# A three-stage kernel on one core: alternating passes of a two-layer graph stage, and one-hot matrices kept in DRAM

## The chip, the core and the metric

The kernel runs on one core of a Trainium2 chip. Its time is the device time of one execution in microseconds (us), and the median of several executions is given. The core has five queues that matter here, each worked off in order. PE is TensorE, with its weight loads shown apart as PEld. DVE is VectorE, ACT is ScalarE, POOL is GpSimd, and SP is SyncE, which issues every DMA of this kernel. An instruction that waits holds up everything behind it on its own queue, and nothing on the others.

## The reference, cut to what matters

The input `x` is 16 graphs x 32 channels x 512 nodes in float32. Three residual parts follow one another: a graph part, a state-space scan, and a low-rank feed-forward part. Only the graph part is touched by the change.

```
keys   = 4 space-filling-curve keys of 3 coordinates (10 bits each)    # per graph
order  = argsort(keys), one order for each of 4 methods
neigh  = for each node i: the 10 nodes around place i in each order    # a window of the sorted list
layer(feats, perm, W_lin, W_conv):
    q      = [center, neigh - center] for 4 methods   -> 256 values per (node, neighbour), as float16
    attn   = softmax(q q^T / sqrt(32)) over the 10 neighbours, 8 heads
    fused  = (attn q) W_lin^T + b;  h = W_conv fused
    return max over neighbours of leaky_relu(instance_norm(h))
f1 = layer(f0, ...)         # 32 channels out
f2 = layer(f1, ...)         # 64 channels out
x += leaky_relu(instance_norm(W_conv3 [f0, f1, f2]))
```

The same orders serve both layers. In layer two only the features differ.

## The kernel before

**The stages.** `graph_part` is emitted first, under an order of work that is written out by hand, then `scan_part`, then `ffn_part`. Both later parts are the same in both kernels.

**The groups and the passes.** Sixteen graphs of 32 channels are four groups g of 128 partitions. A pass is one layer of one group, and there are eight of them in the list `order` (line 955). A pass goes through 43 blocks of 12 nodes (`NG`, `NGRP`). The loop at line 986 emits one block at a time, as a software pipeline: scores of this block, exponentials and sums of the block before, transposed shares and outputs of the block three before, the reduction over neighbours of the block four before, and the differences (POOL, lines 756 to 767) of the block six ahead (`LEAD`). Every third block the differences are copied by four DMAs into `DX` (line 777). A pass of layer two maps to 64 channels and so has twice the columns in `mapped` and twice the outputs and reductions of a pass of layer one.

**The ranks.** `rank_step` compares the keys of 128 nodes with all 512 of their graph: one matmul on PE (line 536) and one signed, accumulated ACTIVATE on ACT (line 537). There are 256 comparisons, 64 for each group. 64 of them are done before the first pass. The loop then emits one in each block (line 999) and a second one until 128 are done (line 1008), so they run through passes 1 to 4.

**The preparation of the next pass.** `prep` (line 622) is a generator, and `steps` (line 965) takes one or two of its steps in each block, beside the blocks of the pass before. `PREP` is the number of steps that it expects, from which it decides between one and two. For layer one `prep` begins with a layer norm (`layernorm_steps`, line 85). It then transposes the features (line 635, tile `pf`), splits them into three bf16 parts, and makes the part of the output that hangs on the center alone (line 656, tile `ph`). Then it orders the features along each sorted list. For each graph b of the group, each quarter c of the nodes and each method m it makes a one-hot matrix `oh` of 128 x 512 from the ranks on DVE (line 720). `place` (line 685) multiplies the three parts with the four one-hot matrices of a (b, c), as 12 matmuls, one step later. After the fourth quarter the result goes through ACT (line 696) to DRAM and from there, laid out anew, to the tile `fs` (lines 700 to 706). The center values go to `crep` in 16 DMAs (line 667). At the end a small DVE copy pads `fs` (line 738). A pass can't begin its differences before its `fs` has landed.

**The tails.** `end` (line 915) closes a pass with norms and leaky ReLU; for layer two `finish` (line 941) adds a matmul, a layer norm and the residual. These steps are taken from the fourth block of the next pass on, ahead of the steps of `prep`.

Of the kernel before, what the change touches and what calls it, by code (L numbers as in the profile page):

```python
# [8 lines left out]
F32 = mybir.dt.float32  # L9
F16 = mybir.dt.float16  # L10
BF16 = mybir.dt.bfloat16
# [34 lines left out]
NHT = 16  # L46
LR = 18
LEAD = 6
PREP = 45


@with_exitstack
def kernel(ctx: ExitStack, tc: tile.TileContext, I, out):
    nc = tc.nc
    const = ctx.enter_context(tc.tile_pool(name="const", bufs=1))
    dram = ctx.enter_context(tc.tile_pool(name="dram", bufs=1, space=DRAM))

    id32 = const.tile([P, P], F32, name="id32")
    make_identity(nc, id32)
    ones = const.tile([P, P], F32, name="ones")  # L60
    nc.vector.memset(ones, 1.0)


    xt = const.tile([P, NBG, D], F32, name="xt")

    def rstd_steps(pool, dst, var, k, key):

        t = pool.tile([P, k], F32, tag="rs_t", name=f"rst_{key}")
        nc.vector.tensor_scalar(t, var, EPS, None, ALU.add)
        s = pool.tile([P, k], F32, tag="rs_s", name=f"rss_{key}")  # L70
        nc.scalar.activation(s, t, AF.Ln)  # L71
        r = pool.tile([P, k], F32, tag="rs_r", name=f"rsr_{key}")
        nc.scalar.activation(r, s, AF.Exp, scale=-0.5)  # L73
        yield
        h = pool.tile([P, k], F32, tag="rs_h", name=f"rsh_{key}")
        nc.vector.tensor_tensor(h, r, r, ALU.mult)
        nc.vector.tensor_tensor(h, h, t, ALU.mult)
        nc.vector.tensor_scalar(h, h, -0.5, 1.5, ALU.mult, ALU.add)
        nc.vector.tensor_tensor(dst, r, h, ALU.mult)

    def rstd(*args):
        for _ in rstd_steps(*args):
            pass

    def layernorm_steps(pool, dst, src, key):

        st = pool.tile([P, 6], F32, tag="ln_st", name=f"lnst_{key}")
        nc.vector.bn_stats(st, src)
        mv = pool.tile([P, 2], F32, tag="ln_mv", name=f"lnmv_{key}")
        nc.vector.bn_aggr(mv, st)  # L90
        r = pool.tile([P, 1], F32, tag="ln_r", name=f"lnr_{key}")
        yield from rstd_steps(pool, r, mv[:, 1:2], 1, key)
        nc.vector.tensor_scalar(dst, src, mv[:, 0:1], r, ALU.subtract, ALU.mult)

    def layernorm(*args):
        for _ in layernorm_steps(*args):
            pass

    U = const.tile([P, NBG, D], F32, name="U")

    def scan_input(pool, sq, q):


        u = U[:, q]
        yield from layernorm_steps(pool, u, xt[:, q], f"s{q}")
        nc.vector.tensor_tensor(xt[:, q], xt[:, q], u, ALU.add)
        ms = pool.tile([P, 1], F32, tag="ms", name=f"ms{q}")
        nc.scalar.activation(sq, u, AF.Square, accum_out=ms)
        yield
        nc.vector.tensor_scalar(ms, ms, 1.0 / D, None, ALU.mult)  # L110
        r = pool.tile([P, 1], F32, tag="msr", name=f"msr{q}")
        yield from rstd_steps(pool, r, ms, 1, f"ms{q}")
        nc.vector.tensor_scalar(u, u, r, None, ALU.mult)
        yield


    nc.scalar.preload_act_table_set("natural_log_exp_and_others")
    with ExitStack() as cx:
        graph_part(nc, tc, cx, I, dram, id32, ones, xt, U, layernorm_steps, rstd_steps, scan_input)
    late = ctx.enter_context(tc.tile_pool(name="late", bufs=1))  # L120
    lows = LowRank(nc, tc, late, I)
    with ExitStack() as cx:
        scan_part(nc, tc, cx, I, id32, ones, xt, U, rstd, lows)
    with ExitStack() as cx:
        ffn_part(nc, tc, cx, I, id32, xt, layernorm, lows, out)
# [248 lines left out]
def graph_part(nc, tc, cx, I, dram, id32, ones, xt, F0, layernorm_steps, rstd_steps, scan_input):  # L374
# [244 lines left out]
    def later_tile(n):  # L619
        return ps_1.tile([P, D], F32, tag="misc", bufs=2, name=f"kd{n}")  # L620

    def prep(g, layer, delay=1):


# [2 lines left out]
        src = F1[g] if layer else F0[:, g]  # L627
        if layer == 0:
            yield from layernorm_steps(sm, src, xt[:, g], f"g{g}")
        dC = dram.tile([P, D], F32, name=f"dC{key}")  # L630
        nc.sync.dma_start(out=dC, in_=src)

# [50 lines left out]
        pend = []  # L683

        def place():
            b, c, ohs, pp = pend.pop()
            for m, oh in ohs:
                for k in range(3):
                    nc.tensor.matmul(  # L689
                        pp[32 * m:32 * m + 32, :], lhsT=F3[k][:, c, 32 * b:32 * b + 32], rhs=oh,  # L690
                        start=(c == 0 and k == 0), stop=(c == 3 and k == 2),
                    )
            if c < 3:
                return
            so = wk.tile([P, D], F32, tag="so", name=f"so{key}_{b}", bufs=2)
            nc.scalar.copy(so, pp)
            dS = dram.tile([P, D], F32, name=f"dS{key}_{b}")

            def store():
                nc.sync.dma_start(out=dS, in_=so)  # L700
                later.append([3, spread])

            def spread():
                for m in range(M):
                    r = 32 * b + 8 * m
                    nc.sync.dma_start(
                        out=fs[r:r + 8, :, :D], in_=dS[32 * m:32 * m + 32].rearrange("(h c) n -> c h n", h=4)
                    )

            later.append([2, store])  # L710

        for b in range(4):
            while ranked[0] < ranks_of(4 * g + b):
                yield False
            pp = None
            for c in range(4):
                ohs = []
                for m in range(M):
                    oh = wk.tile([P, D], BF16, tag="oh", name=f"oh{key}_{b}_{m}_{c}", bufs=8)
                    nc.vector.tensor_scalar(  # L720
                        oh, it2, rank[:, c, m, 4 * g + b:4 * g + b + 1], None, ALU.is_equal
                    )
                    ohs.append((m, oh))
                    if m == 1:
                        tick()
                        yield
                if pend:
                    place()
                if c == 0:
                    pp = ps_1.tile([P, D], F32, tag="pp", name=f"pp{key}_{b}")  # L730
                pend.append((b, c, ohs, pp))
                tick()
                yield
        place()
        while later:
            tick()
            yield
# [203 lines left out]
    def finish(g, F2):  # L941
        p3 = ps_1.tile([P, D], F32, tag="misc", bufs=2, name=f"p3_{g}")
        for j, f in enumerate((F0[:, g], F1[g], *F2)):
            nc.tensor.matmul(p3, lhsT=W3[:, j], rhs=f, start=(j == 0), stop=(j == 3))
        h3 = wk.tile([P, D], F32, tag="h3", name=f"h3_{g}", bufs=1)
        nc.scalar.copy(h3, p3)
        yield
        n3 = wk.tile([P, D], F32, tag="n3", name=f"n3_{g}", bufs=1)
        yield from layernorm_steps(sm, n3, h3, f"f{g}")
        yield  # L950
        nc.vector.scalar_tensor_tensor(n3, n3, 0.2, n3, ALU.mult, ALU.max)
        nc.vector.tensor_tensor(xt[:, g], xt[:, g], n3, ALU.add)

    made = {}
    order = [(0, 0), (1, 0), (0, 1), (1, 1), (2, 0), (3, 0), (2, 1), (3, 1)]
    keys = [f"{layers[layer][0]}_{g}" for g, layer in order]
    first = prep(*order[0], 18)
    next(first)
    for _ in first:
        if ranked[0] < FIRST:  # L960
            rank_step(early_tile)
# [3 lines left out]
    def steps(at, gi):  # L965


        if tails:
            if next(tails[0], tails) is tails:
                tails.pop(0)  # L970
            return
        if at + 1 >= len(order):
            return
        if at + 1 not in ahead:
            if at > 0 and gi < 4:
                return
            ahead[at + 1] = [prep(*order[at + 1]), PREP]
        a = ahead[at + 1]
        for _ in range(2 if a[1] > NGRP - LEAD - 1 - gi else 1):
            if next(a[0], None) is False:  # L980
                break
            a[1] -= 1

    ahead = {}
    blocks = [(at, gi) for at in range(len(order)) for gi in range(NGRP)]
    for it in range(len(blocks) + 4):
# [9 lines left out]
        do(turn, 3)  # L996
        do(scores, 0)
        do(reduce, 4)
        rank_step(later_tile)
        do(greatest, 0)  # L1000
        do(mapped, 0)
        do(sums, 1)
# [1 line left out]
            tails.extend(scan_input(sm, junk(q), q) for q in range(NBG - 1))  # L1004
        steps(at, gi)
        do(shares, 1)
        if ranked[0] < 8 * 4 * M:
            rank_step(later_tile)
        do(outputs, 3)
        if it + LEAD < len(blocks):  # L1010
            to, g2 = blocks[it + LEAD]
            if g2 == 0:
                for _ in ahead[to][0]:
                    pass
            differences(to, g2)
    for t in (*tails, scan_input(sm, junk(NBG - 1), NBG - 1)):
        for _ in t:
            pass
# [381 lines left out]
```

## Time and profile before

| what | value |
|---|---|
| median of 3 runs | 2449.3 us (2441.37 to 2454.86) |
| the profiled execution | 2442.78 us |
| its span, first to last instruction | 2440.9 us |
| graph part: start, eight passes | 0 to 103.1 us, 103.1 to about 1380 us |
| scan and feed-forward parts | about 1380 to 2440.9 us |
| PE busy over the span | 2135.6 us (87%) |
| DVE busy over the span | 1739.5 us (71%) |
| ACT busy over the span | 1098.7 us (45%) |
| POOL busy over the span | 830.9 us (34%) |
| share of the 16 DMA engines, SP's queue | 21.6% |

Blocks and passes can be told apart in the trace by the first matmul of each block, the one of line 802: there are 344 of them, 43 to a pass, and their starts give the time of each block. The shares over the whole span mix passes of two layers with the two later parts, so what bounds the graph part has to be read pass by pass. The chain that ended last is no help here: it is followed back only as far as the last few per cent of the span, all of it in the feed-forward part.

### The profile page before, as it was taken

What the parts mean: (1) busy time and instruction counts of PE and PEld (TensorE: products, weight loads), DVE (VectorE), ACT (ScalarE), POOL (GpSimd) and SP (SyncE); (2) the same over time, 40 slices, a digit from 0 to 9 for tenths busy, and PEclk for the clock granted to TensorE, in tenths of its full rate; (3) what the DMA queues carried; (4) which work ended last, traced back from release to release, by engine and by line L of the source; (5) the groups of instructions that cost most, each with busy time, mean ns of one, the idle gap of its engine ahead of it and who ended that gap; (6) DMA issues with size and microseconds to landing.
All of it is one profiled execution on the core that took longest, in us unless ns stands there. A gap on an engine that the chain in (4) does not pass through costs nothing. (4 is left out here: it accounts for less than half of the span.)

```text
span 2440.9 us, 88578 instructions
## 1 busy us (share of the span) xinstructions
PE 2135.6 (87%) x39025; PEld 1247.9 (51%) x39146; DVE 1739.5 (71%) x3718; ACT 1098.7 (45%) x2023; POOL 830.9 (34%) x897
## 2 busy tenths in 40 slices
PE   5479677999899677879998879999999999999979
PEld 2145455667667454566777634444444444444422
DVE  8379798888899889988999866653554626455643
ACT  5567556666665334454555322332333424333331
POOL 2056556445446556564655400020211202021200
PEclk9889999999999899999999889999999999999989
DMA  2232232221122233322211222213122131310000
GB/s 48 60 65 65 57 74 61 58 59 44 43 62 59 52 73 65 72 52 67 58 34 40 63 73 75 75 31 95 52 61 65 39 86 31 87 57 22 26 35 17
DMA packets 121624, 137.98 MB, mean 57 GB/s; under 512 B 18398, under 2 KB 79506, under 8 KB 121154
## 3 DMA queue, kind: packets, MB, share of 16 engines
q1 hardware_dynamic: 121240, 132.32, 21.6%
q8 instruction: 307, 5.03, 0.9%
q14 instruction: 77, 0.63, 0.1%
HBM read 77.02 MB, written 12.85 MB: 37 GB/s over the span
## 5 line engine op out<-in xcount | busy, mean ns | idle before, releaser
L846 POOL TENSOR_TENSOR EN<-e,rz 128x480 f32<-128x480 f32 x344 | 342.3, 995 | 561.4 <-DVE rz L844 424.1
L871 PE MATMUL u<-WA,DD 128*32 128x128 bf16 (+1 forms) x16512 | 421.6, 251 | 51.1 <-issue 34.2
L871 PEld LDWEIGHTS <-DD 128*32 128x32 f16 x16512 | 341.1, 99 | 69.8 <-issue 66.0
L876 ACT COPY us<-u 128x512 f32<-128x512 f32 x516 | 301.9, 586 | 151.9 <-PE u L871 133.6
L831 ACT ACTIVATE e<-s,smc 128x480 f32<-128x480 f32 x344 | 227.2, 660 | 287.0 <-PE s L826 253.4
L767 POOL TENSOR_TENSOR DD<-fs,crep 128x480 f16<-128x480 f32 (+2 forms) x344 | 349.5, 1017 | 0.0
L890 PE MATMUL h<-e,us 128*32 128x30 f32 (+1 forms) x11008 | 286.1, 211 | 58.2 <-DVE e L852 23.9
L890 PEld LDWEIGHTS h<-e,us 128*32 128x32 f32 (+1 forms) x11008 | 253.2, 127 | 143.8 <-issue 53.5
L1098 DVE SCALAR_TENSOR_TENSOR cyh<-ppch,t_conv_w,cyh 128x496 f32<-128x496 f32 (+2 forms) x192 | 137.5, 716 | 221.6 <-ACT cyh L1093 217.6
L818 DVE TENSOR_REDUCE c<-s 128x16 bf16<-128x480 f32 x344 | 219.6, 638 | 73.2 <-PE s L809 70.4
L1247 PE MATMUL po<-wo,gs 128*128 128x512 f32 x512 | 240.5, 605 | 10.5 <-DVE xt L1250 10.3
L1174 POOL TENSOR_TENSOR da<-lei,dA 128x512 f32<-128x512 f32 x32 | 40.5, 1268 | 612.0 <-PE pl L1179 577.6
L1086 PE MATMUL ppch<-hT,winch 128*128 128x512 f32 x512 | 232.2, 593 | 0.0
L1086 PE MATMUL ppg<-hT,wing 128*128 128x512 f32 x512 | 231.9, 593 | 0.0
L852 DVE STREAM_TRANSPOSE e<-EN 128x512 f32<-128x512 f32 x344 | 224.5, 653 | 0.6 <-POOL EN L846 0.6
L838 DVE TENSOR_REDUCE z<-e 128x16 f32<-128x480 f32 x344 | 219.4, 638 | 0.0
L537 ACT ACTIVATE sgn<-kd 128x512 bf16<-128x512 f32 x256 | 153.0, 598 | 73.9 <-PE kd L536 44.9
L809 PE MATMUL s<-DX,DD 128*32 128x120 f16 x5504 | 144.5, 224 | 33.8 <-DMA DX<-DD 27.4
L809 PEld LDWEIGHTS <-DD 128*32 128x32 f16 x5504 | 82.3, 97 | 178.3 <-issue 133.6
L720 DVE TENSOR_SCALAR oh<-it,rank 128x512 bf16<-128x512 f16 x512 | 166.9, 386 | 7.8 <-PE pp L689 7.8
L1086 PEld LDWEIGHTS ppch<-hT,winch 128*128 128x128 f32 x512 | 93.6, 190 | 122.7 <-issue 122.4
L826 PE MATMUL s<-c,idb 128*128 128x480 bf16 x344 | 131.5, 382 | 28.4 <-DVE c L818 26.8
(323 smaller groups left out, 2746.0 us busy)
## 6 DMA issues: line engine op xcount, KB each, us to landing
DX<-DD SPq DMA_DIRECT2D x456, 90.0 KB
wo<-in_out_proj SPq DMA_DIRECT2D x64, 256.0 KB
wing<-in_in_proj SPq DMA_DIRECT2D x64, 256.0 KB
winch<-in_in_proj SPq DMA_DIRECT2D x64, 256.0 KB
dS<-so SPq DMA_DIRECT2D x32, 256.0 KB
fs<-dS SPq DMA_DIRECT2D x128, 64.0 KB
crep<-dC SPq DMA_DIRECT2D x128, 64.0 KB
wincB<-in_in_proj SPq DMA_DIRECT2D x8, 256.0 KB
```

Of the source, the lines that this page charges most:

```text
L767: nc.gpsimd.tensor_tensor(d[:, :, m0 - n0:n1 - n0], win, crep[:, :, m0:n1].unsqueeze(3).to_broadcast([P, 4, n1 - m0, K]), ALU.subtract,)
L809: nc.tensor.matmul(s[rh, j * 4 * QB:(j + 1) * 4 * QB].rearrange("p (b q) -> p b q", b=4), lhsT=d[:, h, c0:c0 + 32], rhs=dx[:, h, :, c0:c0 ...
L818: nc.vector.tensor_reduce(c, live["s", at, gi].rearrange("p (i q) -> p i q", q=QB), AX.X, ALU.max, negate=True)
L831: nc.scalar.activation(e, s.rearrange("p (i q) -> p i q", q=QB), AF.Exp, scale=smc)
L838: nc.vector.tensor_reduce(z, e, AX.X, ALU.add)
L846: nc.gpsimd.tensor_tensor(en[:, :, :QB], e, rz.unsqueeze(2).to_broadcast([P, NI, QB]), ALU.mult)
L852: nc.vector.transpose(e.rearrange("p i q -> p (i q)"), en.rearrange("p i q -> p (i q)"))
L871: nc.tensor.matmul(u[rh, jj], lhsT=d[:, h, c0:c0 + 32], rhs=WA[k][:, h].rearrange("p b o -> p (b o)"), start=(jj == 0 and k == 0), stop=(k ...
L876: nc.scalar.copy(us[:, j - jj:j + 1], u)
L890: nc.tensor.matmul(h[r:r + co, pr, q0:q0 + QB], lhsT=us[:, j, b * co:(b + 1) * co], rhs=e[:, 4 * j + b, :QB], start=True, stop=True,)
L1086: nc.tensor.matmul(pp, lhsT=w[:, k], rhs=hT[:, k], start=(k == 0), stop=(k == 3))
L1247: nc.tensor.matmul(po, lhsT=gs[:, i, q * P:(q + 1) * P], rhs=wo[i], start=(i == 0), stop=(i == TG - 1))
```

## The change

Four things are changed, all of them in the graph part.

1. **The order of the passes.** Groups 1 and 2 change places in the middle: group 2's first layer comes before group 1's second. Before, the layers ran 1 1 2 2 1 1 2 2; after, 1 1 2 1 2 1 2 2.
2. **One-hot matrices kept.** For groups 1 and 2 (`KEPT`) the one-hot matrices that layer one makes are stored to DRAM, two methods to a tile of 256 KB, 32 stores for a group. Layer two of these groups makes none: it loads them, 32 loads of 256 KB for a group. A load is emitted at the end of its block. `place` then works two quarters behind instead of one, so the load of a quarter reuses the buffers that `place` read two quarters before. The buffers are 4 of 2 KB a partition instead of 8 of 1 KB.
3. **The comparisons.** They are limited by `wanted`: 64 in each of the passes that run layer one of groups 0, 1 and 2 (the first, the second and the fourth pass). In the first pass three are emitted in each of the first 8 blocks and two after that; in the other two passes one, and two in every other block.
4. **Smaller steps.** `layernorm_steps` gives way after its statistics, `prep` after its layer norm, and `finish` before its last addition. The expected numbers of steps are 48, 45 and 30 for layer one, layer two, and layer two from kept matrices.

```diff
-PREP = 45
+PREP = (48, 45, 30)
...
         nc.vector.bn_stats(st, src)
+        yield
         mv = pool.tile([P, 2], F32, tag="ln_mv", name=f"lnmv_{key}")
...
+    KEPT = (1, 2)
+    kept = {}
+    transfers = []
...
             yield from layernorm_steps(sm, src, xt[:, g], f"g{g}")
+            yield
...
         def place():
-            b, c, ohs, pp = pend.pop()
-            for m, oh in ohs:
+            b, c, ohs, pp = pend.pop(0)
+            for m in range(M):
                 for k in range(3):
                     nc.tensor.matmul(
-                        pp[32 * m:32 * m + 32, :], lhsT=F3[k][:, c, 32 * b:32 * b + 32], rhs=oh,
+                        pp[32 * m:32 * m + 32, :], lhsT=F3[k][:, c, 32 * b:32 * b + 32], rhs=ohs[m // 2][:, m % 2],
...
             for c in range(4):
-                ohs = []
-                for m in range(M):
-                    oh = wk.tile([P, D], BF16, tag="oh", name=f"oh{key}_{b}_{m}_{c}", bufs=8)
-                    nc.vector.tensor_scalar(
-                        oh, it2, rank[:, c, m, 4 * g + b:4 * g + b + 1], None, ALU.is_equal
-                    )
-                    ohs.append((m, oh))
-                    if m == 1:
+                if c == 0:
+                    pp = ps_1.tile([P, D], F32, tag="pp", name=f"pp{key}_{b}")
+                at_hand = layer == 1 and g in KEPT
+                if at_hand and len(pend) == 2:
+                    place()
+                ohs = [
+                    wk.tile([P, 2, D], BF16, tag="oh", name=f"oh{key}_{b}_{c}_{i}", bufs=4) for i in range(2)
+                ]
+                for i, oh in enumerate(ohs):
+                    if at_hand:
+                        transfers.append((oh, kept[g, b, c, i]))
+                        continue
+                    for j in range(2):
+                        m = 2 * i + j
+                        nc.vector.tensor_scalar(
+                            oh[:, j], it2, rank[:, c, m, 4 * g + b:4 * g + b + 1], None, ALU.is_equal
+                        )
+                    if layer == 0 and g in KEPT:
+                        kept[g, b, c, i] = dram.tile([P, 2, D], BF16, name=f"k{key}_{b}_{c}_{i}")
+
+                        def keep_it(to=kept[g, b, c, i], oh=oh):
+                            nc.sync.dma_start(out=to, in_=oh)
+
+                        later.append([1, keep_it])
+                    if i == 0:
                         tick()
                         yield
-                if pend:
+                if pend and not at_hand:
                     place()
-                if c == 0:
-                    pp = ps_1.tile([P, D], F32, tag="pp", name=f"pp{key}_{b}")
                 pend.append((b, c, ohs, pp))
                 tick()
                 yield
-        place()
+        while pend:
+            place()
+            tick()
+            yield
...
         nc.vector.scalar_tensor_tensor(n3, n3, 0.2, n3, ALU.mult, ALU.max)
+        yield
         nc.vector.tensor_tensor(xt[:, g], xt[:, g], n3, ALU.add)
...
-    order = [(0, 0), (1, 0), (0, 1), (1, 1), (2, 0), (3, 0), (2, 1), (3, 1)]
+    order = [(0, 0), (1, 0), (0, 1), (2, 0), (1, 1), (3, 0), (2, 1), (3, 1)]
...
-    next(first)
+    for _ in range(4):
+        next(first)
...
-            ahead[at + 1] = [prep(*order[at + 1]), PREP]
+            g, layer = order[at + 1]
+            ahead[at + 1] = [prep(g, layer), PREP[layer + (layer == 1 and g in KEPT)]]
...
+    def wanted(at):
+
+        return ranks_of(4 * min(NBG, 1 + sum(layer == 0 for _, layer in order[:at + 1])) - 1)
...
-        rank_step(later_tile)
+        if ranked[0] < wanted(at):
+            rank_step(later_tile)
...
-        if ranked[0] < 8 * 4 * M:
+        if ranked[0] < wanted(at) and (at == 0 or gi % 2):
             rank_step(later_tile)
         do(outputs, 3)
+        if at == 0 and gi < 8:
+            rank_step(later_tile)
...
             differences(to, g2)
+        for oh, of in transfers:
+            nc.sync.dma_start(out=oh, in_=of)
+        transfers.clear()
```

## The prediction

> **What bounds it.** I read the table of busy times by stretch first, one stretch for each pass (columns: length, then busy us of PE, PEld, DVE, ACT and POOL with instruction counts, granted TensorE clock, DMA share, GB/s).
>
> ```profile
> core 0: us, PE busy (x) PEld busy (x) DVE busy (x) ACT busy (x) POOL busy (x), PEclk, DMA share, GB/s
> 103.10:279.70 176.60, 127.24 (x4382) 75.01 (x4392) 123.30 (x277) 104.47 (x244) 91.74 (x109) 0.88 0.29 66
> 279.70:425.30 145.60, 111.13 (x4418) 75.33 (x4457) 129.75 (x286) 87.57 (x181) 86.38 (x96) 0.95 0.28 66
> 425.30:597.00 171.70, 159.37 (x4420) 118.89 (x4457) 146.05 (x335) 113.01 (x224) 86.14 (x96) 0.99 0.25 56
> 597.00:771.40 174.40, 162.64 (x4424) 121.30 (x4451) 155.00 (x367) 105.68 (x206) 85.86 (x95) 0.98 0.23 53
> 771.40:924.70 153.30, 113.46 (x4421) 77.04 (x4420) 137.54 (x317) 58.48 (x101) 86.01 (x96) 0.93 0.29 62
> 924.70:1066.90 142.20, 106.41 (x4415) 71.56 (x4414) 129.77 (x286) 58.43 (x96) 86.45 (x96) 0.96 0.30 65
> 1066.90:1226.30 159.40, 152.88 (x4416) 116.50 (x4414) 146.93 (x335) 83.61 (x138) 86.23 (x96) 0.98 0.24 58
> 1226.30:1380.00 153.70, 143.88 (x4216) 112.31 (x4214) 145.24 (x334) 83.06 (x154) 79.59 (x82) 0.99 0.17 37
> ```
>
> The heavy passes (layer two: the third, fourth, seventh and eighth row) have PE busy 93 to 96% of their length: PE sets their time. The light passes (second, fifth, sixth) have DVE at 89 to 91% and PE at 74 to 76%: there DVE comes first and PE has 35 to 40 us to spare. The rest of the span, 1380 to 2441, is not touched. So work that leaves PE in a heavy pass counts in full, and work put on PE in a light pass is partly covered. (The page has 136 of the 256 comparisons as PE records, so PE's column reads a little low where they run.)
>
> **Comparisons.** Three stretches of nine blocks (34 to 42 of a pass) without preparation, PE alone: the third pass with a comparison in each block, then the fourth and the seventh without.
>
> ```profile
> 560.60:593.40 32.80, 30.53 (x884) 1.00 0.21 46
> 738.70:768.20 29.50, 29.50 (x895) 1.00 0.27 63
> 1194.20:1223.10 28.90, 28.90 (x884) 1.00 0.22 51
> ```
>
> (32.8 - 28.9) / 9 = 0.43 us for a comparison in a heavy pass. 43 stand in the third pass and 31 in the fourth; all leave: -18.5 and -13.3. They come back in light passes. A light pass with 43 of them took 145.6, one with none 142.2, so 3.4 / 43 = 0.08 each while DVE is in front; uncovered, 0.43. The second pass gets 21 more: between 2 and 9, I take 3, since DVE still leads there. The first pass loses 11: -2. The new fourth pass gets 64, treated below. ACT has room: 58 busy of 150, plus 64 x 0.8 (598 + 196 ns rows).
>
> **One-hots no longer made.** The same table for tile `oh` alone (PE's and DVE's columns), in the two light passes that prepare with 64 of them:
>
> ```profile
> 771.40:924.70 153.30, 17.04 (x192) 21.79 (x64) 0.93 0.29 62
> 924.70:1066.90 142.20, 18.35 (x192) 23.19 (x64) 0.96 0.30 65
> ```
>
> So 22 us of DVE go in each of two passes, and the new order puts both (preparing group 1's and group 2's second layer) inside light passes, the fourth and the sixth, where DVE is in front. What is late next is PE. Sixth pass: like the old fifth (light, with the tail of a heavy pass): 153.3 - 22 = 131, and 5 less for a stall told below: 126; PE's 113.5 lies under that. Fourth: the same 126 by DVE, but PE now has 113.5 + 64 x 0.4 = 139; with 3 us of idle left, 142.
>
> **Loads in their place.** No load of this kind stands in the trace. The nearest rows are on SP's queue (start, us, then the DMA and how many):
>
> ```profile
> 321.18 7.83 SPq L667 DMA_DIRECT2D crep<-dC  x16
> ...
> 355.76 0.54 SPq L700 DMA_DIRECT2D dS<-so  x1
> 359.20 1.31 SPq L706 DMA_DIRECT2D fs<-dS  x4
> ```
>
> A 256 KB store issued at 355.76 released the dependent load at 359.20: 3.4 us. An issue costs SP about 0.45. A quarter's two loads wait on SP until `place` of two quarters before has read the buffers. Where two steps are taken in a block, the next `place` comes after PE's work of one block, some 2.3 us (light, without comparison 2.0, with 1.5 of them 2.6); the load is there after 0.9 + 3.4 = 4.3: PE waits 2 us. The order of instructions shows four blocks with two quarters each. SP is in order, so the first loads stand behind the 16 `crep` issues, 7.8 us (4 to 8 us of waiting, once), and in one or two blocks behind four `DX` issues, 2.6 us after POOL has finished. Sum: 4 x 2 + 5 + 2 = about 15 for each pass. With one quarter in a block there are two blocks, 6 us, to land in: nothing. Ends: 0 if SP runs ahead everywhere, 40 if every double step also waits behind `DX`. I take 14 and 15: fourth pass 142 + 14 = 156, sixth 126 + 15 = 141.
>
> Here the Trainium skill speaks against the change. "DMA: Bandwidth & Descriptors", section "Anatomy of one DMA", says that a semaphore wait is spent on the issuing sequencer before dispatch, so a waiting load holds all DMAs behind it, and prices a transfer at about 2.0 us + bytes / 436 GB/s: an estimate of 2.6 for 256 KB where the row says 3.4. By the page's price a double step costs 1.2 instead of 2, or 6 us less over both passes. The row is of this queue, so I use it. Its rule to issue early and wait late can't be kept here: with four buffers a load can't be issued before `place`.
>
> **Stores.** 64 more stores, 0.45 of SP each, 8.4 MB a pass: GB/s goes from 66 to about 120, which single fortieths of the second pass already reach. DVE writes a buffer again four steps (two blocks, 7 us) later and must wait for its store. The first stores stand behind `crep`, 7.8 + 0.9 + 3.4 = 12, so DVE waits some 4 us once in each of the first and third passes; I take 3 each, ends 0 and 8.
>
> **Norm steps.** Two lines of the view of waits (us in total, times, longest):
>
> ```profile
> PE pf L635 <- DVE U L93: 9.7, 2, 5.0
> ...
> DVE fs L738 <- DMA fs<-dS: 31.3, 2, 19.9
> ```
>
> The first line (waits of PE in the fourth and fifth passes) says that the transposes of a fresh layer norm hold PE 5 us in each. Now the statistics and the logarithm stand a block earlier, and DVE has 1.3 us left to do before the transposes: 2 us of wait stay. The new third and fifth passes are heavy and prepare layer one, so they have it; the new fourth and sixth don't (the 5 us above). The second line (DVE, first pass) is the wait for `fs`; 19.9 belongs to the start, 11.4 to the end of the pass, since ranks come late there. Ranks now come faster and `place` ends four blocks earlier; other passes wait 4 to 5.5: -5.
>
> **The sum,** against the profiled execution (span 2440.9, time 2442.8):
>
> - first: 176.6 - 5 - 2 + 3 = 172.6
> - second: 145.6 + 3 = 148.6
> - third: 171.7 - 18.5 + 3 + 2 (norm wait, new here) = 158
> - fourth 156, from above
> - fifth: the old fourth without 31 comparisons and 3 us of norm wait, 174.4 - 13.3 - 3 = 158; the old seventh, 159.4, says the same
> - sixth 141, from above
> - seventh and eighth: 159.4 - 1 and 153.7 - 1 for the smaller steps
>
> 1245 against 1277, so -32: 2411. The median of the runs shown is 6.5 higher than that execution, so the forecast is **2418**; its own range is 2400 to 2436.
>
> **Rivals.**
>
> - *The loads are hidden* (25%). SP runs ahead of PE and the stalls of 29 us fall away, or overlap the waits on DVE that light passes have anyway: 2418 - 29 = 2389. For it: SP issues little; its instructions take below half of a light pass. Against it: buffers for two quarters only.
> - *The light passes don't follow DVE* (12%). If the round trip scores, maximum, exponential, sum, share, transpose bounds them, taking 22 us from DVE saves 8. That gives back 28: 2446, no change. For it: blocks without one-hots at the start of the second pass still take 2.9 us. Against it: DVE at 77 of 80 us where one-hots are made (320 to 400).
> - *The wait moves to SP* (16%), slower. In the fourth and sixth passes each double step waits for the four `DX` issues and for POOL before them, 0.9 + 3.4 + 2.6 - 2.3 = 4.6 us; eight such quarters and the start make 40 us a pass instead of 14.5: 2418 + 51 = 2469. It decides from 30 us a pass, where the whole gain is used up. For it: every third block has a `DX` copy in the same queue. Against it: only every third, and SP doesn't wait for the first of them.
>
> The forecast has 47%. About 0.5%, 12 us, is what a measurement of this kernel can tell from no change: faster is below 2437. Faster: 0.47 x 0.97 + 0.25 + a tenth of 0.12 = 0.72; slower 0.15; the rest 0.13. The range is 2382 to 2462: it takes in the hidden loads and the no-change case, and leaves out most of the slow one.
>
> **What would show it.** In heavy passes without preparation, blocks of 3.2 us everywhere. DVE without `oh` in passes four and six, and PE waiting for `oh` loads in the blocks with two quarters, 10 to 20 us a pass. `pf` waits near 2. DVE waits on stores below 5 us a pass. Light passes four and six near 156 and 141. I am wrong if PE's waits for loads are nothing or above 30 us a pass, or if the fourth pass is above 165.

## The result, and the profile after

| kernel | median | runs | ratio to before (95% interval) |
|---|---|---|---|
| before | 2449.8 us | 4 | |
| after | 2474.5 us (2471.4 to 2480.4) | 4 | 1.0106 (1.0081 to 1.0131) |

The change made the kernel about 1% slower: 25 us by the medians, where 31 us less had been forecast. The table of busy times by stretch has, for the fourth and the sixth pass of the kernel after (columns as before):

```profile
core 0: us, PE busy (x) PEld busy (x) DVE busy (x) ACT busy (x) POOL busy (x), PEclk, DMA share, GB/s
...
590.00:767.70 177.70, 138.27 (x4468) 81.03 (x4486) 118.07 (x245) 99.29 (x228) 85.35 (x95) 0.92 0.39 101
...
925.50:1104.40 178.90, 117.91 (x4423) 79.10 (x4422) 118.65 (x246) 59.10 (x100) 85.87 (x96) 0.89 0.39 98
...
```

These are the light passes that prepare layer two from loads. They were to take 156 and 141 and take 177.7 and 178.9, together 60 us more. DVE did lose its work there (118 busy instead of the 137 of a light pass that makes one-hots), and PE is busy 78% and 66% of these passes (20 of the 64 comparisons of the fourth pass are missing from PE's records, so the 78 reads 4 to 5 points low). Nothing is full, so something is waited for. The view of PE's waits in the sixth pass (total us, times, longest) begins:

```profile
PE pp L695 <- DMA oh<-k: 29.9, 7, 17.2
PE s L850 <- DVE c L842: 7.4, 8, 1.4
```

The first line is `place` waiting for one-hots that are still being loaded, 29.9 us in one pass and 17.2 in one piece. In the fourth pass the same line reads 19.4 us in 10 waits. How the 17.2 came about is seen by laying SP's timeline beside PE's (start, us, instruction; in brackets the idle time and what ended it). First SP, where a group's length includes the waits inside it:

```profile
981.59 15.93 SPq L801 DMA_DIRECT2D DX<-DD  x8
997.56 8.48 SPq L673 DMA_DIRECT2D crep<-dC  x16
1006.56 10.60 SPq L1051 DMA_DIRECT2D oh<-k  x8
```

And PE:

```profile
995.34 0.85 PE L895 MATMUL u<-WA,DD 128*32 128x128 bf16 x48
1013.35 3.03 PE L695 MATMUL pp<-oh,F 128*32 128x512 bf16 x22 [17.16 <-DMA oh<-k]
```

PE comes to the first `place` at 996. At that time SP is still in `DX` and then issues `crep`, 16 DMAs in 8.5 us. The first load is issued at 1006.6, and PE goes on at 1013.3, 6.8 us later.

This wait costs more than its length. The table by stretch has, for the 3 us after this wait and for the 3.6 us after those:

```profile
1013.35:1016.40 3.05, 3.05 (x32) 2.18 (x33) 0.00 (x0) 0.00 (x0) 0.00 (x0) 0.50 0.40 124
1016.40:1020.00 3.60, 3.57 (x110) 1.97 (x107) 1.99 (x4) 1.25 (x2) 0.35 (x1) 0.96 0.77 261
```

The granted clock (third column from the end) was 1.00 in the 6 us before the wait, 0.50 right after it and 0.96 again 3 us later. The matmuls of `place`, which stand behind the waits, are busy for 24.3 and 22.0 us in the fourth and sixth passes; in a kernel whose `place` waits for no load (traffic_only, below) the same number takes 15.3 and 14.8. What the slower clock costs in all was not measured.

### The profile page after: what moved, and what is told of

Read it like the earlier page. It is cut to its first block, busy times and chain, and to the rows that moved or that the text cites. A ratio compares the mean times of both kernels' runs of the same rounds, so it can differ in the third digit from the quotient of the medians.

```text
span 2472.3 us, 88737 instructions
## 1 busy us (share of the span) xinstructions
PE 2160.7 (87%) x39099; PEld 1249.3 (51%) x39146; DVE 1701.3 (69%) x3590; ACT 1091.6 (44%) x2023; POOL 830.6 (34%) x897
## 5 line engine op out<-in xcount | busy, mean ns | idle before, releaser
L895 PEld LDWEIGHTS <-DD 128*32 128x32 f16 x16512 | 341.0, 98 | 53.5 <-issue 49.3
L914 PE MATMUL h<-e,us 128*32 128x30 f32 (+1 forms) x11008 | 288.2, 212 | 44.0 <-DVE e L876 24.3
L1284 PE MATMUL po<-wo,gs 128*128 128x512 f32 x512 | 240.5, 605 | 10.4 <-DVE xt L1287 10.3
L695 PE MATMUL pp<-oh,F 128*32 128x512 bf16 x1536 | 130.1, 399 | 53.1 <-DMA oh<-k 49.3
```

Source lines behind the costliest of these rows:

```text
L895: nc.tensor.matmul(u[rh, jj], lhsT=d[:, h, c0:c0 + 32], rhs=WA[k][:, h].rearrange("p b o -> p (b o)"), start=(jj == 0 and k == 0), stop=(k ...
L914: nc.tensor.matmul(h[r:r + co, pr, q0:q0 + QB], lhsT=us[:, j, b * co:(b + 1) * co], rhs=e[:, 4 * j + b, :QB], start=True, stop=True,)
L1284: nc.tensor.matmul(po, lhsT=gs[:, i, q * P:(q + 1) * P], rhs=wo[i], start=(i == 0), stop=(i == TG - 1))
```

## The experiments

The expectations name two sides. Theory Q says that what was lost is the wait for loads, made by the order of issues on SP, so another place for the loads or for `crep` wins it back. Its rivals say that the loss lies in something that no order mends: in the traffic itself, in light passes that don't follow DVE, in the new order of passes or in the comparisons. Each edit is against the kernel after. Lengths of passes are differences of starts of first matmuls, from one profiled execution each. That execution can lie off the median of its kernel, by 10.5 us below in late_single and 7.0 above in late_first at most, so differences of some us between passes are not firm, and the medians are given beside them. The seventh pass, whose work is alike in all of these kernels, varies from 157.5 to 160.4. The first takes 171 to 177 with stores and 164 to 167 without (176 to 177 with the old comparisons, and 220.5 with the cut matmuls). The last four rows are, like no_keep, without keeping:

```
pass              1      2      3      4      5      6      7    ratio to before
before          176.6  145.6  171.7  174.4  153.3  142.2  159.4  (layers 1 1 2 2 1 1 2)
after           170.8  148.9  166.8  177.7  157.8  178.9  158.7  1.0106
no_keep         166.6  146.8  161.8  155.0  157.0  153.3  160.3  0.9908
store_only      175.5  150.5  167.7  154.2  156.0  153.9  158.5  0.9942
nothing_made    163.6  150.4  162.3  144.4  157.2  145.3  159.4  0.9814
traffic_only    172.0  151.1  165.3  155.7  161.9  155.6  159.2  0.9980
crep_late       176.9  150.5  165.5  175.9  157.4  177.1  157.5  1.0109
late_first      171.4  149.4  163.3  166.6  157.7  169.9  158.9  1.0012
late_single     177.0  147.6  163.0  167.2  157.0  160.9  159.4  1.0050
act_loads       173.9  149.1  164.5  172.6  156.5  165.1  159.5  1.0052
act_spread      173.4  150.8  163.6  166.4  158.0  163.5  160.2  1.0038
plain_cmp       176.4  146.4  169.6  151.7  156.8  153.4  158.8  0.9964
big_steps       164.3  149.1  163.7  153.0  165.0  149.3  159.0  0.9923
old_order       165.3  146.6  160.1  172.0  153.6  141.5  159.9  0.9896
no_keep_split   220.5  195.6  162.0  194.6  158.0  200.9  160.4  1.0673
```

### Without keeping: no stores, no loads

```diff
-    KEPT = (1, 2)
+    KEPT = ()
```

> The changed kernel without kept one-hots (KEPT is empty): layer two of groups 1 and 2 makes its one-hots on DVE again; new order of passes, comparisons and norm steps stay. Theory Q (TensorE waits for loads that stand late in SP's queue, and this alone makes the change slow): blocks 20 to 31 of the fourth and sixth passes, 75 and 78 us with loads, fall to about 46 each as in the old fifth pass, and the stores' 8 us go: 2474 - 29 - 32 - 8 = about 2405, below the kernel before by 45. Theory C (the comparisons moved to light passes and the new order cost what they save): 2440 or more, no faster than before. Theory L (light passes don't follow VectorE): 2405 or less too, but the fourth and sixth passes gain no more than the waits.

2422.7 us, ratio 0.9908 (0.9884 to 0.9932). Layer two makes its one-hots on DVE again, and the fourth and sixth passes take 155.0 and 153.3, together 48 us less than with loads. Theory Q expected 2405, 18 us less. Still the whole loss is in keeping the one-hots; the rest of the change is a gain of 0.9%.

### The stores alone

```diff
-                at_hand = layer == 1 and g in KEPT
+                at_hand = False
...
-            ahead[at + 1] = [prep(g, layer), PREP[layer + (layer == 1 and g in KEPT)]]
+            ahead[at + 1] = [prep(g, layer), PREP[layer]]
```

> The stores of the one-hots stay, the loads go: layer two makes them anew. Theory Q: within 10 us of the kernel without kept one-hots (about 2413), since the stores only hold VectorE 3 to 5 us in the first and third passes. Theory S (the stores, 16.8 MB and 64 issues on SP, cost as much as the loads): 2440 or more.

2430.5 us, 0.9942 (0.9926 to 0.9958). By the medians the 64 stores cost 7.8 us, as Q expected (within 10). The loads instead of making then cost the step from 0.9942 to 1.0106, some 40 us.

### Putting `crep` or the loads elsewhere in SP's queue

The late `crep`, issued 18 quarter steps later, after the last load:

```diff
-        later.append([delay, copies])
+        later.append([18 if layer == 1 and g in KEPT else delay, copies])
```

> The changed kernel, but in the two preparations with loads the 16 crep DMAs are issued after the last load instead of ahead of the first. Theory Q: the first wait of TensorE in the fourth and sixth passes (17 us in the sixth) loses the 8.5 us of crep issues each, so about 2474 - 17 = 2457. Theory B (the buffers' round trip from place to load to place makes the waits, wherever other DMAs stand): 2474 within 5.

2471.8 us, 1.0109 (1.0085 to 1.0132): no gain, and a miss of Q. PE's waits for loads fell only from 49.3 to 37.0 us over the run, and the time came back later in the passes: in a block of 11.9 us in the fourth, in which SP issues the late copies and PE waits 5.7 us for a load, and in one of 13.0 in the sixth, in which DVE waits 11.4 us for `fs`.

The same, with the loads issued before the block's differences and their `DX` copies:

```diff
         steps(at, gi)
+        for oh, of in transfers:
+            nc.sync.dma_start(out=oh, in_=of)
+        transfers.clear()
         do(shares, 1)
...
             differences(to, g2)
-        for oh, of in transfers:
-            nc.sync.dma_start(out=oh, in_=of)
-        transfers.clear()
```

> As crep_late, and the loads of a block are emitted ahead of the differences of the same block, so that the DX copies, which wait for GpSimd and take 2.6 to 3.9 us to issue, stand behind them. Theory Q: another 10 us less, about 2447, with PE's wait for oh below 20 us in all. Theory B: 2474 within 5, since with 4 buffers the loads still wait for place.

2447.9 us, 1.0012 (1.0001 to 1.0024). The waits for loads fell to 15.3 us and the time by 24, as Q expected here: the order on SP is worth that much. The two passes still take 28 us more than with one-hots made on DVE (by the medians the whole kernel takes 25 more than without keeping, the stores' 7.8 among them).

And with `PREP` 26 instead of 30 for kept matrices, so that a block takes one quarter and two blocks lie between a load and its use:

> As late_first (crep last, loads ahead of the differences), but the preparation with loads expects 26 steps in place of 30, so that one quarter is taken in each block from the 20th on and none has two. Theory B (what waits are left in late_first, 15 us on TensorE, are the round trip place, load, place of the blocks with two quarters): waits for oh under 5 us, total about 2435. Theory D (the loads slow the passes by their traffic, which delays instruction fetches): within 5 of late_first, 2448.

2457.9 us, 1.0050 (1.0033 to 1.0067), above what either theory expected (2435 and 2448). Waits for loads 8.4 us; but the slower pace puts the end later, and DVE's view of waits for the fourth pass shows what is late next:

```profile
DVE fs L762 <- DMA fs<-dS: 12.2, 1, 12.2
```

### The loads on another queue

`nc.sync` becomes `nc.scalar` for the loads, emitted before the differences as above, `PREP` 26:

> The changed kernel with the loads issued by ScalarE's queue right after the step that placed, in place of SP's queue at the end of the block, and one quarter a block from the 20th on (26 steps). crep stays ahead of them on SP, where it no longer matters. Theory Q (the loads' cost is where they stand in SP's queue, and moving crep back only moved the wait to fs): waits for oh under 5 us, no late fs, the fourth and sixth passes within 4 us of those with nothing loaded (144 and 145): 2399 + 8 for stores + 5 = about 2412, faster than without kept one-hots. Theory D (the loads' traffic itself delays TensorE's instruction fetches): 2440 or more although TensorE doesn't wait for oh.

2459.1 us, 1.0052 (1.0038 to 1.0066). Theory Q expected 2412. PE waits only 3.1 us for loads in the whole run, and yet the two passes take 29 us more than without loads. SP's timeline in the fourth pass:

```profile
656.03 3.55 SPq L801 DMA_DIRECT2D DX<-DD  x4
659.68 21.70 SPq L673 DMA_DIRECT2D crep<-dC  x16
681.47 7.13 SPq L801 DMA_DIRECT2D DX<-DD  x8
```

The same 16 issues that spread over 8.5 us now spread over 21.7, beside the loads, and the next `DX` copies stand behind them. One by one in the trace, each issue takes 0.26 to 0.48 us in both kernels; what grew is the time that SP stands between them, up to 4.2 us at once. The first of PE's waits in that pass says who pays:

```profile
PE s L833 <- DMA DX<-DD: 11.1, 1, 11.1
```

The wait for `oh` has become one for `DX`. The Trainium skill says in "DMA: Bandwidth & Descriptors", section "Issuing engines are not separate DMA queues", that DMAs started by the scalar, sync or gpsimd engine run on the same 16 DMA engines. The run fits that: another queue took the loads out of SP's order, not out of SP's way. That this sharing is what SP stands for between its issues is not shown.

With `crep` also spread in the two preparations with loads, one copy for each quarter step:

```diff
-        later.append([delay, copies])
+        for n in range(16):
+            def copy(r=8 * n, b=n // 4):
+                nc.sync.dma_start(out=crep[r:r + 8], in_=...)
+            later.append([1 + n, copy])
```

> As act_loads (loads on ScalarE's queue, one quarter a block), but the 16 crep DMAs of a preparation with loads are issued one a quarter instead of all at once. In act_loads TensorE waited only 3 us for oh, but 11 us once in the fourth pass for DX copies that stood on SP behind crep, whose 16 issues took 23 us beside the loads. Theory Q (a standing in a queue is what costs, now DX behind crep): that block of 16 us falls to 3 in the fourth and sixth passes, 172.6 and 165.1 become about 155 and 150, total about 2430. Theory D (the loads' traffic slows whatever is issued beside them): 2450 or more, the wait only shows elsewhere.

2451.5 us, 1.0038 (1.0019 to 1.0058), where Q expected 2430. The 11-us wait is gone and smaller ones stand in its place. SP's waits in the fourth pass have these:

```profile
SPq L811 <- DMA oh<-k: 11.0, 4, 5.0
SPq L681 <- DMA oh<-k: 10.0, 4, 3.3
```

The issues of `DX` (L811) and `crep` (L681) are ended by the landing of loads that another engine issued. That this is a shared path of the DMAs, and not a semaphore taken for it by the inference, the trace doesn't prove.

### What making and loading are worth at all

Two kernels that leave part of the work out put bounds on it. In the first nothing is stored or loaded, and in the preparation of layer two of groups 1 and 2 nothing is made either: `place` multiplies with a fixed tile.

```diff
-                        transfers.append((oh, kept[g, b, c, i]))
                         continue
...
+                    still if at_hand else wk.tile([P, 2, D], BF16, tag="oh", ...)
```

> Leaves work out: nothing is stored or loaded, and the preparations of group 1's and group 2's second layer multiply with a fixed tile in place of their one-hots, on the schedule of the changed kernel. So the fourth and sixth passes have neither the 64 one-hots on VectorE nor any load. Theory V (VectorE bounds light passes, as forecast): 22 us less in each than without kept one-hots (155 and 153 us, 2423 in all): about 2379. Theory F (TensorE's own instruction fetch bounds them: in the changed kernel's sixth pass a 16 KB fetch comes about every 3.6 us, a light block has some 202 TensorE instructions of 256 in a fetch, so 2.83 us a block): about 7 us less in each, 2409, with the fourth and sixth passes at 146 or more.

2399.4 us, 0.9814 (0.9794 to 0.9834), between the two theories and nearer to F. The two passes take 289.7 us; with one-hots made on DVE (no_keep) they take 308.3. So the two passes are 9.3 us shorter each, though DVE is busy 17.6 and 17.7 us less. (By the medians the kernels differ by 23 us, with an interval of about 8 either way.) That is the most that loads could win on this schedule.

It is not all the price of making. A preparation that makes nothing expects 30 steps instead of 45 and so ends earlier: its last `place` stands in the 32nd block instead of the 36th. In no_keep the last `fs` is late, as DVE's view of waits in the sixth pass says:

```profile
DVE fs L762 <- DMA fs<-dS: 8.5, 1, 8.5
```

In the fourth pass the line reads 6.8, and with nothing made 0 and 0.6. The block in which DVE waits (the 39th) takes 7.9 and 10.0 us in no_keep, 2.2 and 3.4 with nothing made: 12.3 of the 18.6 us. Some 3 us a pass are left for the one-hots themselves.

Where DVE's relief went is read from PE's waits in the sixth pass, here for no_keep:

```profile
PE h L914 <- DVE e L876: 13.1, 8, 7.7
PE s L850 <- DVE c L842: 12.1, 11, 1.4
...
PE u L895 <- issue: 2.0, 3, 0.9
PE h L914 <- issue: 1.1, 1, 1.1
```

and here with nothing made:

```profile
PE s L851 <- DVE c L843: 8.1, 9, 1.4
PE u L896 <- issue: 7.5, 8, 1.7
PE h L915 <- issue: 5.7, 6, 1.6
PE h L915 <- DVE e L877: 5.4, 7, 1.4
...
PE s L834 <- issue: 2.8, 2, 1.7
```

The two waits on DVE fell from 25.2 to 13.5, by 12 (6.3 of it in the longest one, behind the late `fs`); PE's idle time with no visible cause ("issue") rose from 3.1 to 16.0, by 13. What DVE gave back, something inside PE took. This holds for the sixth pass. In the fourth the same two waits fell from 12.1 to 3.8 and PE, with 64 comparisons, had less to wait for.

The second kernel stores and loads as the change does, but layer two's `place` multiplies with the fixed tile, so nothing waits for the loads:

```diff
-    rhs=ohs[m // 2][:, m % 2],
+    rhs=still[:, m % 2] if layer == 1 and g in KEPT else ohs[m // 2][:, m % 2],
```

> Leaves out part of the result: the changed kernel with its stores and loads, each issued on SP where the change has it, but the place of the two preparations with loads multiplies with a fixed tile, so that nothing waits for a load, and a load waits for no place. Theory Q (waiting for the loads is what costs): the fourth and sixth passes fall to 5 us above those with nothing loaded (144 and 145), about 2415 in all. Theory D (SP's issue and the DMA engines' work on 8.4 MB a pass delay DX, fs and the rest): they stay 15 us or more above, 160 each, 2440 in all.

2442.7 us, 0.9980 (0.9964 to 0.9996). That is near theory D's 2440, though the passes lie 11 and 10 us above those with nothing made, not 15. They take 155.7 and 155.6, together 311.3: the traffic alone costs 21.6 us over nothing made, more than the 18.6 of making. The medians say so too: the ratio is 0.9980, against 0.9942 for store_only, which has the same stores and makes its one-hots. Its PE waits in the sixth pass hold a line that stands at 0.3 us with nothing made:

```profile
PE s L835 <- DMA DX<-DD: 9.4, 2, 4.7
```

and SP's timeline shows the place:

```profile
990.66 6.21 SPq L1053 DMA_DIRECT2D oh<-k  x8
996.92 2.90 SPq L803 DMA_DIRECT2D DX<-DD  x4
```

The `DX` copies that followed `crep` directly at nothing made now follow 8 loads, and PE stands until 1002.7. In the sixth pass this explains 9.4 of the 10.3 us; in the fourth the same line has 4.6 of 11.3. The granted clock was 0.96 there against 0.99 with nothing made; what that explains of the rest stays open.

### What PE does with the time

In the kernel after, the last 11 blocks of the sixth pass, without any preparation, take 2.83 us each although DVE needs only 2.4 and PE is busy for 1.9. PE pauses eight times there, every 3.3 to 4.7 us; six of the pauses, of 0.9 to 1.6 us, are put to "issue". The DMA view of that stretch (1073.3 to 1104.4) has a queue that is not the kernel's (packets, MB, share):

```profile
q8 instruction: 8, 0.13, 1.9%
```

Each packet is 16 KB. Passes have 34 or 35 of them for some 8800 to 9000 PE instructions (matmuls and weight loads), one for about 256. A packet at 1083.53 took 0.99 us, and PE stood from 1085.24 to 1086.13; each of the eight pauses begins within 0.8 us of the end of one of the eight packets. The last 27 to 32 us of the sixth pass in before, nothing_made and traffic_only have 7, 8 and 8 packets, and each has its pause too. In the seventh pass of before, a heavy one, the last 7 packets have none, so a packet by itself doesn't stop PE. (The sum in the expectations, 202 / 256 x 3.6 = 2.84 us a block, is no evidence: with one packet for 256 instructions, the packets keep the pace of the blocks, whatever sets it.) If the supply of instructions sets the pace, more instructions for the same columns must cost time. The experiment cuts each mapping matmul of layer one in two halves of 64 columns, 96 more PE instructions a block, without keeping:

```diff
+                    parts = 2 if npair == 1 else 1
+                    w = 4 * co // parts
+                    for o in range(parts):
                         nc.tensor.matmul(
-                            u[rh, jj], ...
+                            u[rh, jj, o * w:(o + 1) * w], ...
```

> The kernel without kept one-hots, but in layer one's passes each of the 48 matmuls of the mapping is cut into two of 64 columns: the same columns in all, 96 more instructions a block with their weight loads (298 in place of 202). Theory F: light blocks without preparation go from 2.83 to 298 / 256 x 3.6 = 4.2 us, so 40 to 55 us more in each of four light passes: about 2600. Theory V: VectorE's 2.3 us a block and TensorE's columns stay the same, and the added 48 weight loads of 4 rows at a time take TensorE up to 0.4 us: within 20 us, about 2440.

2608.1 us, 1.0673 (1.0657 to 1.0688), as theory F expected. Light passes grew by 40 to 54 us, heavy ones, whose instructions are as before, by 0 to 1. The DMA view of the sixth pass has 34 instruction packets for no_keep, and for the cut matmuls, with PE's waits below:

```profile
q8 instruction: 50, 0.82, 1.8%
```

```profile
PE u L898 <- issue: 36.8, 28, 2.0
PE h L918 <- issue: 17.0, 10, 3.1
PE s L833 <- issue: 8.2, 5, 2.0
```

16 more packets, as 43 x 96 / 256 says; 62 us of "issue" in place of 3.1, and of the 25.2 us of waits on DVE for `e` and `c` 2.7 are left. PE's busy time grew too, by 17 us (132.6 against 115.3, since a half takes more than half the time), less than the pass, which grew by 48. A light pass is near the rate at which PE gets its instructions. That the pauses are the fetches themselves rests on how they lie in time; whether the packets or something else that goes with each 256 instructions sets the rate, no run here separates.

### The other parts of the change, without keeping

Comparisons spread as before (one in each block, two until 128):

```diff
-        if ranked[0] < wanted(at):
-            rank_step(later_tile)
+        rank_step(later_tile)
...
-        if ranked[0] < wanted(at) and (at == 0 or gi % 2):
+        if ranked[0] < 8 * 4 * M:
```

(and without the third one in the first 8 blocks)

> Without kept one-hots and in the new order, but with the comparisons as in the kernel before: one in each block and two until 128 are done, through the first four passes, of which the third is heavy. Theory Q as forecast: the third pass gets 43 comparisons at 0.43 us, +18 there; the second loses 21 and the fourth about 33 at 0.1 to 0.2, -7 together: about 2434. If comparisons cost in light passes what they cost in heavy ones: within 5 of 2423.

2436.0 us, 0.9964 (0.9947 to 0.9982), near the 2434 expected, so the new schedule is worth 13.3 us: by passes 9.8 in the first, where a block of 12.8 us at the end goes, 7.8 in the third, and -3.3 in the fourth.

Steps as large as before (without the three new yields, `PREP` 46 for layer one):

> Without kept one-hots and without the three added yields of the norm steps (46 steps expected for layer one). Theory N, as forecast: TensorE's wait for the transposes of a layer norm goes from 2.7 back to 5 us in the third and fifth passes, and tails are a block shorter: 4 to 6 us more than without kept one-hots, about 2428. Rival: nothing, 2423 within 3, because the added blocks of the tails take back what the shorter waits give.

2425.8 us, 0.9923 (0.9901 to 0.9946). 3 us above no_keep, with overlapping intervals: not decided. The fifth pass is 8 us longer, the sixth 4 shorter.

The order of the passes as before, comparisons still in the passes of layer one of groups 0, 1 and 2 (three or two a block in the fifth, as in the first; this part of the edit is left out here):

```diff
-    order = [(0, 0), (1, 0), (0, 1), (2, 0), (1, 1), (3, 0), (2, 1), (3, 1)]
+    order = [(0, 0), (1, 0), (0, 1), (1, 1), (2, 0), (3, 0), (2, 1), (3, 1)]
```

> Without kept one-hots and with the passes in the order of the kernel before (layers 1 1 2 2 1 1 2 2). The comparisons still stand in three light passes: the first, the second and, three or two a block, the fifth, where group 3's preparation waits for them. Theory O (the order itself gives nothing; it is only what lets comparisons and loads stand in light passes): within 6 us of 2423. If the order itself is worth the 10 us by which the new order with the old comparisons beats the kernel before: about 2433.

2418.0 us, 0.9896 (0.9864 to 0.9929), as no_keep within the intervals. No gain of the order by itself is seen. Both kernels beat the one before and the one after; which of the two is better is not decided.

## Why the prediction was wrong

Two steps failed, one in the sixth pass, the other in the fourth and the sixth.

**"So 22 us of DVE go in each of two passes ... What is late next is PE."** The step failed in the sixth pass. Without its loads that pass was to take 126 us, with PE's 113.5 lying under it; with nothing made or loaded it took 145.3, 19 us more. In the fourth, where PE with its comparisons was put in front, 142 were forecast and 144.4 measured: there the step held.

The relief itself was smaller. The 64 one-hots fill 22.5 us as a row of their own in no_keep, but DVE's busy time falls by only 17.7 without them, since the spans of successive DVE instructions overlap in the trace (their sum is 157.7 us in that pass, DVE busy 137.1). And PE was late next, but not by its busy time. PE's column showed 113 of 153 us and I took the rest for spare. Part of it is time in which PE stands with no cause that the profile shows. The kernel before has it already; its waits of PE in the sixth pass begin:

```profile
PE u L871 <- issue: 10.2, 11, 1.4
PE h L890 <- issue: 9.1, 8, 2.0
```

The step was to save 22 us a pass; removing the one-hots altogether, with no load in their place, saved 9.3 a pass, and two thirds of that is `fs` that no longer comes late. The rival of light passes that don't follow DVE put the saving at 8; that its size came so near is in part luck, and its reason, a round trip of engines, was half of it: in the sixth pass with nothing made 13.5 us of the two waits on DVE remain beside 16.0 of "issue". (Its sum gave 14 us back in both passes; by the prediction's own 142 for the fourth there was nothing to give back in it.)

**"Sum: 4 x 2 + 5 + 2 = about 15 for each pass."** The two passes took 356.6 us against 289.7 with nothing made or loaded: 67 us, 33 a pass, where 29 were forecast for both. This is the larger part of the error: 38 of the 60 us. By traffic_only, 21.6 of them are the traffic and 45.3 the waiting, with the slower PE behind each wait. (The loads of traffic_only don't wait for `place`, so the division is rough.) The sum had no term for the first: the loads delay `DX` on SP's queue, and PE waits for that, about 14 of the 21.6 us. In the second, the starting wait of "4 to 8 us" was 17.2 in the sixth pass, since SP was late with `DX` already before `crep` (in the fourth no single wait passed 5.8); and the time from issue to release, taken as 3.4 us from a lone store, was 6.8 at the place shown, behind 16 copies of `crep`. The 2.6 us that the prediction set beside the 3.4 come from a fit that the Trainium skill ("DMA: Bandwidth & Descriptors", section "Anatomy of one DMA") gives for DMAs issued from GpSimd, so they say little of these loads, which SP issues. Nor had the sum a term for the granted clock of 0.50 after a wait. The waits of PE that were named as the test, 10 to 20 us a pass, came out at 19.4 and 29.9, and the other sign named, a fourth pass above 165, did show. The rival that moves the wait to SP gave 2469, near the 2474 measured, but that is luck in part: it took 40 us of loads a pass instead of 33, and the full saving of 22 on DVE. Its place was only partly right: in the sixth pass the longest wait came at the start, not evenly at each double step.

A part of both errors is one habit: each edit was costed against a single engine or queue, while the freed time of DVE was used up inside PE, and the added DMAs were paid for by `DX`.

The rest held. The comparisons left the heavy passes: the fifth took 157.8 (158 forecast), the seventh 158.7 (158.4). The second took 148.9 (148.6). The first pass lost its stall: 170.8 (172.6). The third took 166.8 instead of 158: DVE's list there has 4.3 us of waits on stores and 4.5 for `fs`, where 3 us were put down for the stores; by the medians the stores cost 7.8 in all (6 forecast). The comparisons are worth less there than -18.5: 7.8 by the experiment. Its steady blocks do gain (3.2 us against 3.6), about 3 us are given back in the two blocks with the wait for `fs` (12.1 against 8.9), and the rest is open. The wait of `pf` was 2.7 us (2 forecast).

## What to carry to other kernels

Before work is taken from the engine that leads a stage, leave that work out altogether and time it: here 22 us of DVE were worth 9.3 a pass at most. Over two passes that is 18.6, less 7.8 for the stores, so loads could win some 11 us of 2450 (15 by the medians), and none of the placements tried won any. An engine that is 75% busy isn't 25% free; look whether its idle time is put to a wait on another engine or to nothing visible, and count its instructions. And DMAs added to a queue are paid for by what stands behind them and beside them, so their price is taken at the place where they run, not from a lone transfer.

## What the hardware showed unexpectedly

- While the kernel runs, a queue of instruction packets moves 16 KB for about every 256 PE instructions. At the end of the sixth pass, without preparation, PE pauses beside each of them (31 packets in four kernels), for 0.9 to 1.6 us in the stretch shown. Cutting the mapping matmuls added 16 packets and 48 us to a pass. Heavy passes have as many packets and next to no such pauses (PE's waits put to "issue": 1.2 us in the seventh pass of before, 20.8 in the sixth).
- A row of issues on SP isn't one price: `crep`'s 16 copies took 8.5 us alone and 21.7 beside loads issued by ACT, with 0.26 to 0.48 us for each issue in both and the rest spent between them.
- After PE's wait of 17.2 us the granted clock was 0.50 for 3 us; after one of 4.7 us (traffic_only, 1002.7 to 1005.6) it was 0.50 for 3 us, too.
- 8.4 MB of loads a pass, at a DMA share of 0.42 to 0.45 instead of 0.28, cost about 11 us a pass without anyone waiting for the data. PE's waits for `DX` account for 9.4 us of it in the sixth pass and 4.6 in the fourth.
